# When a buffer of B and C counts as free in a fused attention and state-space kernel

## The chip, the cores and the metric

The kernel runs on one core of one Trainium2 chip. The metric is device time in microseconds of one execution, and the median of several runs is compared. Everything is float32.

## The reference, cut to what matters

The input is a batch of 4 images with 128 channels of 64 by 64 pixels. Layer 0 is attention with 4 heads of 32 channels over the 4096 pixels of an image, with residual and layer norm. Layer 1 adds a 3 by 3 convolution, a spectral mixing (an FFT, a 1 by 1 convolution, the inverse FFT) and a Mamba block. The Mamba block is where the change sits:

```python
x_dbl = einsum('blr of xs and x_proj_w')
dt = softplus(x_dbl[..., :8] @ dt_proj_w + dt_proj_b)
Bm, Cm = x_dbl[..., 8:24], x_dbl[..., 24:]
# for every pixel t in order, 256 channels d, 16 states n
dA = exp(dt[..., None] * A)
h = dA * h + dt[..., None] * Bt[:, None, :] * xt[..., None]
y = einsum('bdn,bn->bd', h, Ct)
```

B and C are one number for each pixel and state, shared by all channels. The kernel holds channels on the partitions, so each row of B and C has to be copied to all 128 partitions.

## The kernel before

**Tiling.** The pixels are cut into 32 chunks of 512 (L), 8 for each image. Attention runs in 64 halves (HALVES): a chunk of queries and a pair of heads, against 32 tiles of 128 keys (NT). The state space is scanned chunk by chunk, in 32 scans for each chunk: 16 states n times 2 halves of the 256 channels.

**One loop orders everything.** The program is written out by a loop over a step t. Step t of a half makes the scores for one tile of keys, takes their exponentials and multiplies the previous ones with the values; it also makes the scores whose maxima the next half needs (`scores_for_max`, reduced by VectorE on L473). Jobs such as projections, the convolution, normalising and stores are generators that a small planner (`Plan.step`) advances by one piece in a step. The main loop passes t = 2048 when attention ends; the steps after that have only scans and jobs, and this text calls them the tail. All queues run in the order of this text. SP issues nearly all DMAs, one queue for all of them.

**The scan.** A state takes four steps. For scan v of a chunk (v = 2n for the first half of the channels, 2n + 1 for the second) and a step counted from the chunk's start:
- at odd steps, two scans ahead, `scan_input_term` (L845) multiplies B into the input: db. GpSimd does it, VectorE in the tail.
- at even steps, `scan_state` runs the recurrence on VectorE (L857), copies the last column as the carried state (L866, GpSimd), multiplies the result by C (L867, GpSimd) and adds it up (L886 on GpSimd; in the tail TensorE adds through a product with the identity, L893).
- at odd steps, after the input term, the loop may issue one `scan_load`: the rows of B and C of one state, copied to all partitions, 512 KB in one DMA (L823).

The first use of a load is db of the first half (L845), its last use is the product of the second half on L867, "the last product". Load n is first used 3 steps before its first scan, and its last product stands at local step 4n + 2.

**Buffers.** Three buffers named bc go round in turn; `ring[0]` counts the free ones. From step 2017 on, tiles of K and V that attention no longer needs are handed over as well (`spare`), each taking two DMAs (L829); they come back six steps after their last product. `scan_load` takes a ring buffer first. The wait itself is not in this code: the framework makes the DMA wait on SP until the last reader of the buffer, the product on L867, has ended.

**Who stands behind a load on SP.** Every half sends its row maxima through memory: `maxima` stores them (L485) and reads them back one step later as 16 small DMAs (L492, tile MX). `normalise` sends sums of exponentials the same way (L554 and L556, then L559 reading tile zc, VectorE's reciprocal on L562, L564, L567). `flips` loads a partial output into the single buffer ob (L1057) and the mirrored term wr (L994), adds them on GpSimd (L1003, L1004) and stores (L1064). In the text these stand between loads of B and C, as the steps fall.

Of the kernel before, what the change touches and what calls it, by code (L numbers as in the profile page):

```python
# [161 lines left out]
def attention_then_conv_mamba(  # L162
# [21 lines left out]
    NT = N // P  # L184
# [154 lines left out]
    plan = Plan(2, {"x": 2, "f": 1})  # L339
# [114 lines left out]
    def scores_for_max(H, s):  # L454

        k = H % PAIRS
        m, t = divmod(s, TPC)
        assert have["K", k, m] == H // PAIRS // NCH
        if s == 0:
            part[H] = att.tile([P, 2, TPC, NCH], F32, tag="part", name=f"part_{H}")  # L460

        tag = "s2" if H == 0 and s % 2 else "s1"
        sc = psum.tile([P, 2, L], F32, tag=tag, name=f"s1_{H}_{s}")
        for n in range(2):
            for j in range(2):
                nc.tensor.matmul(  # L466
                    sc[:, j, :],
                    QT[H][rows[j], n, t * P : (t + 1) * P],
                    KK[k][m][rows[j], :],
                    start=n == 0,  # L470
                    stop=n == 1,
                )
        nc.vector.tensor_reduce(part[H][:, :, t, m], sc, AX.X, ALU.max)  # L473
# [25 lines left out]
    def scores_for_exp(H, m):  # L499

        k = H % PAIRS
        i, t = divmod(m, TPC)
        assert have["K", k, i] == H // PAIRS // NCH
        s = psum.tile([P, 2, L], F32, tag="s2", name=f"s2_{H}_{m}")
        for n, mov in enumerate((QT[H][:, 0, :], QT[H][:, 1, :], MX[H])):
            for j in range(2):
                nc.tensor.matmul(  # L507
                    s[:, j, :],
                    sel[rows[j], :] if n == 2 else KK[k][i][rows[j], t * P : (t + 1) * P],
                    mov[rows[j], :],  # L510
                    start=n == 0,
                    stop=n == 2,
                )
        e = att.tile([P, 2, L], F32, tag="e", name=f"e_{H}_{m}", bufs=3)
        nc.scalar.activation(e, s, AF.Exp)  # L515
        es[H, m] = e

    def times_values(H, m):

        k = H % PAIRS  # L520
        i, t = divmod(m, TPC)
        assert have["V", i] == H // PAIRS // NCH
        if m == 0:
            po[H] = psum.tile([P, L], F32, tag="o", name=f"po_{H}")
        e = es.pop((H, m))
        for j in range(2):
            nc.tensor.matmul(  # L527
                po[H][used[j], :],
                VA[i][:, t, 2 * k + j, :],
                e[:, j, :],  # L530
                start=m == 0,
                stop=m == NT - 1,
            )
        if m == NT - 1:
            p = po.pop(H)
            oz[H] = att.tile([P, L], F32, tag="oz", name=f"oz_{H}", bufs=1)
            nc.scalar.activation(oz[H][used[0], :], p[used[0], :], AF.Identity)
            nc.vector.tensor_copy(oz[H][used[1], :], p[used[1], :])  # L538
# [271 lines left out]
    spare = [((HALVES - 1) * NT + 1, KK[0][i : i + 2]) for i in range(0, NCH, 2)]  # L810
    spare += [(HALVES * NT + 12, KK[1][i : i + 2]) for i in range(0, NCH, 2)]
    spare += [(HALVES * NT + 20, VA[i : i + 2]) for i in range(4, NCH, 2)]
    taken, ring = {}, [3]

    def flat(t):
        return t.bitcast(F32) if len(t.shape) == 2 else t.rearrange("p t h d -> p (t h d)")[:, :L]

    def scan_load(c, n):

        if ring[0]:  # L820
            ring[0] -= 1
            bc = loc.tile([P, 2, L], F32, tag="bc", name=f"bc_{c}_{n}", bufs=3)
            nc.sync.dma_start(bc, bcds[c][n::NS, :].partition_broadcast(P))  # L823
            bcs[c, n] = [bc[:, k, :] for k in range(2)]
        else:
            taken[c, n] = spare.pop(0)[1]
            bcs[c, n] = [flat(t) for t in taken[c, n]]
            for k in range(2):
                nc.sync.dma_start(  # L829
                    bcs[c, n][k].unsqueeze(1),  # L830
                    bcds[c][k * NS + n : k * NS + n + 1, :].partition_broadcast(P),
                )

    def scan_decay(c, v):
        n, hf = divmod(v, NH)
        k = hf * NS + n

        tag = "o" if plan.t >= HALVES * NT + 2 and v % 2 else "dA"
        dA[c, v] = psum.tile([P, L], F32, tag=tag, name=f"dA_{c}_{k}")
        nc.scalar.activation(dA[c, v], dts[c][hf], AF.Exp, scale=negA[:, k : k + 1])  # L840

    def scan_input_term(c, v, engine):
        n, hf = divmod(v, NH)
        db[c, v] = loc.tile([P, L], F32, tag="db", name=f"db_{c}_{hf * NS + n}")
        engine.tensor_tensor(db[c, v], us[c][hf], bcs[c, n][0], ALU.mult)  # L845

    def scan_state(c, v):

        n, hf = divmod(v, NH)
        k = hf * NS + n  # L850
        assert (c, hf) in scaled
        late = plan.t > HALVES * NT + 1
        if late:
            hs = flat(VA[v % 4])
        else:
            hs = loc.tile([P, L], F32, tag="hs", name=f"hs_{c}_{k}")
        nc.vector.tensor_tensor_scan(  # L857
            hs,
            dA.pop((c, v)),
            db.pop((c, v)),  # L860
            state[:, k : k + 1] if c % NCH else zero,
            ALU.mult,
            ALU.add,
        )
        if c % NCH < NCH - 1:
            nc.gpsimd.tensor_copy(state[:, k : k + 1], hs[:, L - 1 :])  # L866
        nc.gpsimd.tensor_tensor(hs, hs, bcs[c, n][1], ALU.mult)  # L867
        if hf == NH - 1 and (c, n) in taken:
            spare.append((plan.t + 6, taken.pop((c, n))))
        elif hf == NH - 1:  # L870
            ring[0] += 1
        if late:

            if c not in sums_late:
                sums_late[c] = psum.tile(
                    [P, NH, L], F32, tag=f"s{1 + c % 2}", name=f"acc_{c}"
                )
            terms = [hs] if n else [xss[c][hf], hs]
            for x in terms:
                waiting.append((plan.t + 4, c, hf, x, n == NS - 1 and x is hs))  # L880
        elif n == 0:
            acc = loc.tile([P, L], F32, tag=f"acc{hf}", name=f"acc_{c}_{hf}")
            accs[c, hf] = acc
            nc.gpsimd.tensor_tensor(acc, xss[c][hf], hs, ALU.add)
        else:
            nc.gpsimd.tensor_tensor(accs[c, hf], accs[c, hf], hs, ALU.add)  # L886
# [217 lines left out]
    t = 6 - SLOT  # L1104
    loaded = 0
    end = (CHUNKS + 3) * SLOT
    while t < end or not plan.idle():
        H, m = divmod(t, NT)
        if 0 <= H < HALVES:
            scores_for_exp(H, m)  # L1110
        h1, s1 = divmod(t + LEAD, NT)
        if 0 <= h1 + 1 < HALVES:
            scores_for_max(h1 + 1, s1)
        H, m = divmod(t - 1, NT)
        last = m == NT - 1
        if last and 0 <= H < HALVES:
            times_values(H, m)
        c, s = divmod(t - LAG, SLOT)
        odd = s % 2 == 1
        if -1 <= c < CHUNKS:  # L1120
            v = c * STATES + s // 2
            if not odd:
                if v >= 0:
                    scan_state(*divmod(v, STATES))
            else:
                if 0 <= v + 1 < CHUNKS * STATES:
                    scan_decay(*divmod(v + 1, STATES))
                if 0 <= v + 2 < CHUNKS * STATES:
                    late = t > HALVES * NT
                    scan_input_term(  # L1130
                        *divmod(v + 2, STATES), nc.vector if late else nc.gpsimd
                    )

                if loaded < CHUNKS * NS and loaded // NS in bcds:
                    if ring[0] or spare and spare[0][0] <= t:
                        scan_load(*divmod(loaded, NS))
                        loaded += 1
        plan.late = t > HALVES * NT
        if plan.late:
            add_states()  # L1140
            if odd:
                plan.step(t, {"D": 4, "P": 4, "A": 6})
            plan.t = t
        elif t < -LEAD:
            plan.step(t, {"D": 4, "P": 4, "A": 4})
        elif odd:
            plan.step(t, {"D": 2, "P": 2, "A": 2})
        else:
            plan.step(t, {"D": 0, "P": 0, "A": 1})
        if not last and 0 <= H < HALVES:  # L1150
            times_values(H, m)
        t += 1
# [76 lines left out]
```

## Time and profile before

| what | value |
|---|---|
| median of 3 runs | 5970.94 us (5969.76 to 5976.89) |
| the profiled execution's own time | 5976.93 us |
| its span, first to last instruction | 5975.1 us |
| TensorE busy | 5766.0 us, 96% of the span |
| GpSimd busy | 4575.5 us, 77% |
| VectorE busy | 4343.8 us, 73% |
| ScalarE busy | 3535.4 us, 59% |
| loads of B and C into bc | 487, 512 KB each |
| DMAs through K and V tiles (L829) | 50, 256 KB each |
| granted TensorE clock | 0.985 over the span |

The span has a start of some 160 us, attention to about 5745 us, and the tail. A table of busy time by stretches gives TensorE 990.40 us of 1000 between 1000 and 2000 us, and 9.94 of 20 between 5760 and 5780 us. So the same wait has a different worth in the two stretches. In the table of waits the idle time of an engine stands before the instruction that ended it, with the instruction or the DMA that released it. SP's own waits are listed apart: standing there costs time only if something behind in its queue is missed by an engine.

### The profile page before, as it was taken

The page shows a single profiled execution, that of the slowest core. Times are in us where ns is not written, and L with a number is a line of the kernel's source. Part 1 is how long each engine was busy: PE and PEld are TensorE (multiplying, and loading weights), DVE is VectorE, ACT ScalarE, POOL GpSimd, SP SyncE. Part 2 cuts the span into 40 slices and gives each one's busy share as a digit, 9 for nine tenths or more (in the row PEclk, how much of TensorE's full clock was granted, in tenths as well). Part 3 has the DMA queues.
Part 4 walks back from the last instruction along what each step waited for, and adds up shares of the span by engine and source line. Part 5 has one row for each costly group of instructions (what it writes and reads, how often), then busy time and mean ns, then how long its engine had stood idle before and what let it go on. Part 6 is the DMA issues. An engine that isn't in the chain of part 4 may idle for free. (4 is left out here: it accounts for less than half of the span.)

```text
span 5975.1 us, 84571 instructions
## 1 busy us (share of the span) xinstructions
PE 5766.0 (96%) x31318; PEld 2461.1 (41%) x31318; DVE 4343.8 (73%) x4633; ACT 3535.4 (59%) x4762; POOL 4575.5 (77%) x4657
## 2 busy tenths in 40 slices
PE   5999999999999999999999999999999999999976
PEld 2444444444444444444444444444444444444422
DVE  4557777777777777777777777777777777777657
ACT  1455666665666665666666666666566666666653
POOL 0006888888888888888788888887888888888887
PEclk7999999999999999999999999999999999999988
DMA  4012232323332222323433333222433322222232
GB/s 126 25 34 59 68 73 74 74 71 110 82 93 75 74 71 72 77 68 83 109 86 79 78 70 71 78 72 68 110 76 94 70 66 66 66 72 66 68 93 88
DMA packets 423324, 456.50 MB, mean 76 GB/s; under 512 B 203360, under 2 KB 204928, under 8 KB 422912
## 3 DMA queue, kind: packets, MB, share of 16 engines
q1 hardware_dynamic: 418256, 449.23, 29.6%
q8 instruction: 247, 4.05, 0.3%
q10 hardware_dynamic: 4656, 1.87, 0.1%
q14 instruction: 165, 1.35, 0.1%
HBM read 376.21 MB, written 66.32 MB: 74 GB/s over the span
## 5 line engine op out<-in xcount | busy, mean ns | idle before, releaser
L473 DVE TENSOR_REDUCE part<-s 128x2 f32<-128x1024 f32 x2048 | 2498.1, 1221 | 1340.5 <-PE s L466 1340.3
L515 ACT ACTIVATE e<-s 128x1024 f32<-128x1024 f32 x2048 | 2095.6, 1023 | 2117.1 <-PE s L507 2114.8
L527 PE MATMUL po<-e,V 128*33 128x512 f32 x8192 | 2182.5, 605 | 4.0 <-DVE oz L538 0.3
L507 PE MATMUL s<-Q,K 64*128 64x512 f32 x8192 | 1502.4, 444 | 12.7 <-ACT e L515 5.7
L466 PE MATMUL s<-K,Q 64*128 64x512 f32 x8192 | 1327.9, 401 | 57.8 <-DVE part L473 46.0
L867 POOL TENSOR_TENSOR hs<-hs,bc 128x512 f32<-128x512 f32 x948 | 1212.6, 1279 | 155.4 <-DVE hs L857 87.1
L507 PEld LDWEIGHTS s<-Q,K 64*128 64x128 f32 x8192 | 610.4, 185 | 1737.9 <-ACT e L515 1290.3
L845 POOL TENSOR_TENSOR db<-u,bc 128x512 f32<-128x512 f32 x948 | 1216.8, 1284 | 0.0
L886 POOL TENSOR_TENSOR acc<-acc,hs 128x512 f32<-128x512 f32 x894 | 1146.7, 1283 | 70.1
L857 DVE TENSOR_TENSOR_SCAN hs<-dA,state,db 128x512 f32<-128x512 f32 x826 | 1052.8, 1275 | 70.3 <-ACT dA L840 39.9
L466 PEld LDWEIGHTS s<-K,Q 64*128 64x128 f32 x8192 | 751.8, 186 | 330.4 <-DVE part L473 165.4
L507 PE MATMUL s<-MX,sel 64*128 64x512 f32 x4096 | 815.4, 393 | 0.0
L840 ACT ACTIVATE dA<-dt,negA 128x512 f32<-128x512 f32 x1024 | 703.3, 687 | 152.7 <-DVE V L857 85.8
L866 POOL COPY state<-hs 128x1 f32<-128x1 f32 x858 | 160.5, 187 | 654.4 <-DVE hs L857 654.4
L527 PEld LDWEIGHTS po<-e,V 128*33 128x33 f32 x8192 | 305.5, 109 | 846.8 <-issue 807.7
L507 PEld LDWEIGHTS s<-MX,sel 64*128 64x128 f32 x4096 | 391.2, 184 | 93.9
L962 PE MATMUL pf<-d,cw 128*128 128x256 f32 x768 | 199.1, 396 | 7.3 <-POOL d L944 7.3
L571 POOL TENSOR_TENSOR op<-op,rz 128x512 f32<-128x512 f32 x32 | 41.5, 1298 | 177.2 <-DMA rz<-rd 177.2
L962 PEld LDWEIGHTS pf<-d,cw 128*128 128x128 f32 x768 | 141.1, 193 | 73.0 <-issue 47.4
L857 DVE TENSOR_TENSOR_SCAN hs<-dA,zero,db 128x512 f32<-128x512 f32 x128 | 163.1, 1275 | 2.9 <-POOL db L845 2.6
L893 PE MATMUL acc<-V,cst 128*128 128x512 f32 x140 | 96.3, 795 | 61.7 <-POOL V L867 61.3
L725 POOL TENSOR_TENSOR xs<-xs,sg_x 128x512 f32<-128x512 f32 x64 | 82.2, 1285 | 74.5 <-ACT sg_x L649 74.5
(156 smaller groups left out, 3541.8 us busy)
## 6 DMA issues: line engine op xcount, KB each, us to landing
bc<-bcd SPq DMA_DIRECT2D x487, 512.0 KB
Q<-qd SPq DMA_DIRECT2D x256, 128.0 KB
K<-kd SPq DMA_DIRECT2D x64, 256.0 KB
MX<-md SPq DMA_DIRECT2D x1024, 0.5 KB
K<-bcd SPq DMA_DIRECT2D x42, 256.0 KB
vd<-vst SPq DMA_DIRECT2D x32, 264.0 KB
V<-vd SPq DMA_DIRECT2D x32, 264.0 KB
xq<-in_x SPq DMA_DIRECT2D x32, 256.0 KB
```

The costliest lines, as they stand in the source:

```text
L466: nc.tensor.matmul(sc[:, j, :], QT[H][rows[j], n, t * P : (t + 1) * P], KK[k][m][rows[j], :], start=n == 0, stop=n == 1,)
L473: nc.vector.tensor_reduce(part[H][:, :, t, m], sc, AX.X, ALU.max)
L507: nc.tensor.matmul(s[:, j, :], sel[rows[j], :] if n == 2 else KK[k][i][rows[j], t * P : (t + 1) * P], mov[rows[j], :], start=n == 0, stop= ...
L515: nc.scalar.activation(e, s, AF.Exp)
L527: nc.tensor.matmul(po[H][used[j], :], VA[i][:, t, 2 * k + j, :], e[:, j, :], start=m == 0, stop=m == NT - 1,)
L840: nc.scalar.activation(dA[c, v], dts[c][hf], AF.Exp, scale=negA[:, k : k + 1])
L845: engine.tensor_tensor(db[c, v], us[c][hf], bcs[c, n][0], ALU.mult)
L857: nc.vector.tensor_tensor_scan(hs, dA.pop((c, v)), db.pop((c, v)), state[:, k : k + 1] if c % NCH else zero, ALU.mult, ALU.add,)
L866: nc.gpsimd.tensor_copy(state[:, k : k + 1], hs[:, L - 1 :])
L867: nc.gpsimd.tensor_tensor(hs, hs, bcs[c, n][1], ALU.mult)
L886: nc.gpsimd.tensor_tensor(accs[c, hf], accs[c, hf], hs, ALU.add)
L962: nc.tensor.matmul(pf[:, k], taps[k][:, dx, :], d[:, k, :, dx : dx + W], start=dx == 0 and not outer, stop=q == 5 or dx == 2 and not outer,)
```

## The change

A ring buffer used to count as free at the text of its last product. Now it carries a due time, four steps behind, and the loop takes it when that time is reached. `ring` becomes a list of due times, three of them long past at the start. Inside the scan part of step t, `plan.t` is still t - 1, on both sides of the comparison.

```diff
-    taken, ring = {}, [3]
+    taken, ring = {}, [-NT] * 3
...
     def scan_load(c, n):
 
-        if ring[0]:
-            ring[0] -= 1
+        if ring and ring[0] <= plan.t:
+            ring.pop(0)
             bc = loc.tile([P, 2, L], F32, tag="bc", name=f"bc_{c}_{n}", bufs=3)
...
         elif hf == NH - 1:
-            ring[0] += 1
+            ring.append(plan.t + 4)
...
                 if loaded < CHUNKS * NS and loaded // NS in bcds:
-                    if ring[0] or spare and spare[0][0] <= t:
+                    if ring and ring[0] <= plan.t or spare and spare[0][0] <= t:
                         scan_load(*divmod(loaded, NS))
                         loaded += 1
```

The number of buffers, the loads, the products and the spare tiles' own rule stay as they are.

## The prediction

> **What bounds the kernel now.** First the page: which engine is full. Then the table of waits, for PE and for SP's queue.
>
> ```profile
> PE 5766.0 (96%) x31318; PEld 2461.1 (41%) x31318; DVE 4343.8 (73%) x4633; ACT 3535.4 (59%) x4762; POOL 4575.5 (77%) x4657
> ```
>
> ```profile
> PE s L466 <- DVE part L473: 46.0, 88, 1.3
> ```
>
> ```profile
> SPq L823 <- POOL hs L867: 2795.0, 421, 29.5
> ```
>
> The last line is what the change aims at: SP stood 421 times, 6.6 us each, before a load whose buffer POOL was still reading. But until about 5745 us PE is 99% busy (990.40 of 1000 us between 1000 and 2000), and PE's stretches of idleness in attention come from DVE's maxima, not from a DMA. So I looked, after the first 480 us, for every idle stretch of a compute engine that a DMA ended. There are five: three for K tiles (L466 on L397, 6.8 us in sum), and two in the tail. The K loads stand behind the store L391, which waits for ACT, not for a B-and-C load; they stay.
>
> The first of the two, by the timelines of SP, DVE and POOL:
>
> ```profile
> 5749.24 1.15 SPq L556 DMA_DIRECT2D op<-oz  x2
> 5762.40 0.39 SPq L823 DMA_DIRECT2D bc<-bcd  x1
> 5762.89 0.41 SPq L559 DMA_DIRECT2D zc<-zd  x1
> ```
>
> ```profile
> 5757.85 0.71 DVE L845 TENSOR_TENSOR db<-u,bc 128x512 f32<-128x512 f32 x1
> 5767.20 0.20 DVE L562 RECIPROCAL zc<-zc 128x8 f32<-128x8 f32 x1 [8.64 <-DMA zc<-zd]
> ```
>
> ```profile
> 5765.39 1.26 POOL L867 TENSOR_TENSOR V<-V,K 128x512 f32<-128x512 f32 x1
> 5769.40 0.70 POOL L866 COPY state<-V 128x1 f32<-128x1 f32 x1 [2.74 <-DVE V L857]
> ```
>
> SP is done with L556 at 5750.39, stands 12 us at a load, and the 4 KB zc goes out at 5762.89. It is 4.31 us on its way, behind 512 KB. DVE idles 8.64 us; POOL has old work until 5766.65 and idles only 2.74. The second one:
>
> ```profile
> 5871.60 0.37 SPq L823 DMA_DIRECT2D bc<-bcd  x1
> 5872.02 0.46 SPq L1064 DMA_DIRECT2D out<-ob  x1
> 5877.48 0.32 SPq L1057 DMA_DIRECT2D ob<-ymd  x1
> 5877.85 0.43 SPq L994 DMA_DIRECT2D wr<-wd  x1
> ```
>
> ```profile
> 5880.84 1.25 POOL L1003 TENSOR_TENSOR ob<-ob,wr 128x504 f32<-128x504 f32 x1 [3.46 <-DMA wr<-wd]
> ```
>
> The store of ob was ready at 5868.17, when L1004 ended, and stood until 5872.02; the next ob can be loaded only when it has landed, and POOL pays 3.46 us.
>
> **The change part by part.**
>
> *Text order.* In the steady part the last product stands at step 4n + 2 and its successor's load at 4n + 3. The due time is (t - 1) + 4, compared with t - 1, at odd steps only: the load moves to 4n + 7. Its first use is at 4n + 9, so a lead of six steps becomes two. Throughput stays: one load in four steps. Counted through the loop, 468 of 512 loads move by 4 steps; at the hand-over to spare tiles some move by 2 or 8, the last 16 by 0 to 4, and ring loads go from 487 to 486. So SP issues as many DMAs as before, one more in two pieces: 0.4 us of SP's own, hidden in its idle time.
>
> *What it takes away.* A moved load finds its product done, so SP no longer stands 2795 us. In attention nothing missed the DMAs behind: worth 0.
>
> In the tail, before zc at step 2051 stands now the load of 2043. Its buffer's product is long done, so it issues behind L556 at about 5750.5, zc at 5750.9, landing (4.3 us again) at 5755.3. DVE needs it at 5758.56: the idle 8.64 goes. But POOL has work until 5766.65 and saves 2.74 us. Its later multiply L571 (op) releases the projection (PE, L586), for which DVE idled 3.29 us before L589 at 5779.15. That chain starts earlier by POOL's 2.74, not by 8.64. What is late next: the load of 2051, now at 2059. It waits for the product of step 2054 (POOL, 5766.65), lands at about 5771.7, and DVE, running ahead, stands some 3 us for it; L589 follows only at 5776.4, so this costs nothing. Value: -2.7; between 0 (if that load lands over 2 us later) and -8.6 (if POOL's queue gave way too).
>
> For the second, the ring has turned by one: the load at 2111 takes the buffer whose product stands at 2106 instead of 2110, so it issues at about 5866.8, the store at 5868.2, ob and wr some 4.5 us earlier than before. POOL's 3.46 goes. Value: -3.5, between 0 and -3.5. Behind it the tail is one chain of DVE and POOL in fixed order, so it passes on. Sum of the tail: -6.2.
>
> *What it moves.* Each ring load is now behind the DMAs of four more steps. Nearly all are harmless: the slack between landing and first use (median 12.5 us before) stays above 5 us in three of four. Once in each half it matters: the load that stood before md and MX now stands behind MX.
>
> ```profile
> 3091.51 0.37 SPq L823 DMA_DIRECT2D bc<-bcd  x1
> 3091.93 0.46 SPq L485 DMA_DIRECT2D md<-neg  x1
> 3096.46 10.37 SPq L492 DMA_DIRECT2D MX<-md  x16
> 3106.89 1.51 SPq L348 DMA_DIRECT2D xq<-in_x  x1
> 3108.51 0.36 SPq L1064 DMA_DIRECT2D out<-ob  x1
> 3108.97 8.70 SPq L823 DMA_DIRECT2D bc<-bcd  x2
> ```
>
> ```profile
> 3110.52 1.29 POOL L845 TENSOR_TENSOR db<-u,bc 128x512 f32<-128x512 f32 x1
> ```
>
> The first row's load is first used at 3110.52. It would now issue at 3108.97 instead of 3091.51, and with the landing of loads in the trace's semaphore updates (median 5.0 us, 4.4 to 6.6 for nine in ten; 5.2 for the one that issued at 3108.97) arrive at 3114.1, 3.6 us late. Done so for all 467 loads before step 2000, 51 are late, 155 us in sum. This bound lets MX stay where it was. But md no longer has a fresh 512 KB ahead of it. An early half, before any such load, shows what that is worth:
>
> ```profile
> 268.49 0.34 SPq L485 DMA_DIRECT2D md<-neg  x1
> 269.96 11.13 SPq L492 DMA_DIRECT2D MX<-md  x16
> ```
>
> 1.47 us from md to MX instead of 4.53: MX comes 3.1 us earlier, in every second half 2 us more, since SP also stood before md there. With MX earlier, the load arrives at about 3111.0, 0.5 us late. Over all loads, with 2.0 us for md, 6 are late by 2.5 us in sum, and some 40 have under 1.5 us to spare.
>
> What lateness costs: db stands three steps ahead of its scan, and in one half of two POOL has gaps that take it up. In the other it has none for some 40 instructions, the delay reaches DVE's scan, the maxima queued behind it, and PE's next scores. Carrying the bound's delays through those rows gives 43 us at DVE and 15 us at PE. Value taken: +1, the 2.5 us being mostly absorbed; between 0 and +43.
>
> *A rule that bears on it.* The trace's 5.0 us can be set against the Trainium skill, page DMA: Bandwidth & Descriptors, section on the anatomy of one DMA: a fixed 2.0 us and bytes over 436 GB/s (fitted on the GpSimd path, while these go through SP). For 524,288 bytes that is an estimate of 3.2 us. By the rule the loads behind MX would be in time and the +1 would be 0; by the trace they are on the edge. The trace is used.
>
> *Sum.* 5975.1 - 6.2 + 1 = 5969.9 span; with the 1.8 us around it 5971.7 in a profiled execution like this one. That one stood 6.0 us above the median shown, so the median would be 5965.7.
>
> **The rivals.**
>
> *A, the forecast*: small tail gain, attention untouched. 5966, on its own between 5959 and 5972.
>
> *B, the tail pays in full.* DVE's 8.64 and POOL's 3.46 are both on the end's path: -12.1, 5958.8, down to 5953 if the copies on L866, 0.65 us beside a busy DVE against 0.18 alone, shorten too. For it: PE is no bound there. Against it: POOL is busy without a gap until 5766.65.
>
> *C, slower: the load behind MX.* One mechanism, once a half: db waits on POOL for a load that issued after 16 small DMAs. If md lands no sooner, +15 - 6.2 = +9: 5980; if all the lateness at DVE reaches PE, +43 - 6.2 = +37: 6008. It decides beyond the 0.2% when the loads of the full halves are late by some 1.2 us each: about 29 such halves must cost PE 0.6 us each, after a slack of about 0.5. For it: the margin is under 1.5 us and two steps are all the lead left. Against it: 1.47 against 4.53 us.
>
> *D, it does nothing*: zc stays late through something else, the other wait too: 5971.
>
> **How the numbers follow.** A measurement of this kernel can tell about 0.2%, 12 us, from no change. A 0.54, D 0.05: within it, 0.59. B 0.23: faster. C 0.18: slower. The range reaches from 5954, in B, to 5983, the lower part of C; about a tenth is left out on the upper side and a little on the lower one.
>
> **What would show it.** SP's wait L823 on L867 falls from 2795 us to under a few hundred, and L492 on md from 246 to about 100-150 us. DVE's 8.64 before L562 and POOL's 3.46 before L1003 are gone; a wait of about 3 us of DVE or less for a bc load appears near 5768. POOL shows few waits of L845 for a bc load in attention, under 1 us each. If they are some 30 to 60 with 2 us or more, and PE's wait for L473 has grown well over 46 us, C is right. If the tail after 5745 us is 10 us shorter or more, B is.

## The result, and the profile after

The changed kernel takes 5961.6 us (median of 14 runs, 5958.31 to 5967.64) against 5973.35 us for the kernel before in the same comparison: a ratio of 0.9981 (95% interval 0.9973 to 0.9989), 11.7 us faster. The profiled execution has a span of 5956.5 us, 18.6 less than the one shown of before; 7 us of that difference are the scatter of single executions.

SP's own waits first, as the table of waits gives them for the changed kernel (waiting line and releaser, us in total, times, longest):

```profile
SPq L823 <- POOL hs L867: 997.3, 159, 29.5
SPq L485 <- DVE neg L482: 568.1, 64, 39.0
SPq L492 <- DMA md<-neg: 72.0, 64, 2.5
```

The last of these rows stood so before:

```profile
SPq L492 <- DMA md<-neg: 246.0, 64, 4.8
```

Standing at a load fell from 2795.0 to 997.3 us. SP now stands at the head of md's chain until VectorE has the maxima ready (L485), and it waits for md before MX 72.0 us instead of 246.0 over 64 halves: 1.1 us each instead of 3.8. Next, where the tail used to wait for zc: SP's timeline, then VectorE's.

```profile
5742.16 1.15 SPq L556 DMA_DIRECT2D op<-oz  x2
5743.40 0.53 SPq L823 DMA_DIRECT2D bc<-bcd  x1
5744.04 0.43 SPq L559 DMA_DIRECT2D zc<-zd  x1
...
5760.50 0.38 SPq L823 DMA_DIRECT2D bc<-bcd  x1
```

```profile
5751.37 0.19 DVE L562 RECIPROCAL zc<-zc 128x8 f32<-128x8 f32 x1
5753.78 0.88 DVE L977 SCALAR_TENSOR_TENSOR ym<-pf,vec,ym 128x256 f32<-128x256 f32 x2 [2.21 <-PE pf L962]
...
5760.78 1.28 DVE L857 TENSOR_TENSOR_SCAN V<-dA,state,db 128x512 f32<-128x512 f32 x1 [1.69 <-PE acc L893]
5765.44 1.21 DVE L845 TENSOR_TENSOR db<-u,bc 128x512 f32<-128x512 f32 x1 [3.38 <-DMA bc<-bcd]
```

zc goes out right behind L556, and the reciprocal has no wait. But most of the 8.64 us comes back as three other waits of VectorE: 2.21 us for the convolution, 1.69 for a scan buffer that TensorE has not added yet, and 3.38 for the load of 5760.50, which the change put behind zc. And the other place, SP and then GpSimd:

```profile
5852.22 0.37 SPq L823 DMA_DIRECT2D bc<-bcd  x1
5853.61 0.34 SPq L1064 DMA_DIRECT2D out<-ob  x1
5858.07 0.32 SPq L1057 DMA_DIRECT2D ob<-ymd  x1
5858.44 1.26 SPq L994 DMA_DIRECT2D wr<-wd  x1
```

```profile
5862.74 1.70 POOL L1003 TENSOR_TENSOR ob<-ob,wr 128x504 f32<-128x504 f32 x1
```

The store is no longer held up by a load, and L1003 starts as soon as GpSimd is free. The price that the prediction looked for is there as well. The page's row of POOL's input term, before and after, and one case of it with the SP rows that lead to it:

```profile
L845 POOL TENSOR_TENSOR db<-u,bc 128x512 f32<-128x512 f32 x948 | 1216.8, 1284 | 0.0
L845 POOL TENSOR_TENSOR db<-u,bc 128x512 f32<-128x512 f32 x946 | 1212.1, 1281 | 6.6 <-DMA bc<-bcd 5.8
```

```profile
1665.14 10.93 SPq L492 DMA_DIRECT2D MX<-md  x16
1676.12 0.59 SPq L348 DMA_DIRECT2D xq<-in_x  x1
1676.80 0.38 SPq L1064 DMA_DIRECT2D out<-ob  x1
1677.22 1.02 SPq L823 DMA_DIRECT2D bc<-bcd  x2
```

```profile
1683.44 1.27 POOL L845 TENSOR_TENSOR db<-u,bc 128x512 f32<-128x512 f32 x1 [1.30 <-DMA bc<-bcd]
```

That is 5.8 us of late loads in the whole of attention. When the instructions of both profiles are laid side by side, this one stands out: the changed kernel's lead shrinks by 1.3 us around 1683 us. The same comparison finds steps of 0.5, 4.0 and 2.2 us in its favour at the three places where one image's keys give way to the next one's, and 11.7 us in the tail (what of this is chance is told below).

Those three places are what the prediction set aside. TensorE waits there for a K tile. Here the middle one, before and after, with the timeline of TensorE, then the busy time by stretches (PEclk, third from the end, is the granted clock):

```profile
2897.60 0.74 PE L466 MATMUL s<-K,Q 64*128 64x512 f32 x4 [3.55 <-DMA K<-kd]
2898.27 2.59 PE L737 MATMUL pd<-xs,xpw 128*64 128x512 f32 x3
```

```profile
2897.60:2901.60 4.00, 4.00 (x11) 1.22 (x12) 1.82 (x2) 0.00 (x0) 1.18 (x1) 0.62 0.79 241
```

```profile
2894.30 0.73 PE L466 MATMUL s<-K,Q 64*128 64x512 f32 x4 [1.23 <-DMA K<-kd]
2894.96 1.50 PE L737 MATMUL pd<-xs,xpw 128*64 128x512 f32 x3
```

```profile
2894.00:2898.00 4.00, 3.70 (x14) 1.32 (x16) 1.82 (x2) 0.72 (x2) 3.73 (x3) 1.00 0.89 229
```

The wait is 2.3 us shorter, and there is a second price that no table of waits shows: behind the long one the granted clock is 0.62 for 4 us, and the same group of matmuls takes 2.59 instead of 1.50 us. Together the place is 4.0 us shorter.

SP's rows that lead to this tile, a load of B and C, the reads of Q and the K tile, before and then after:

```profile
2884.36 0.37 SPq L823 DMA_DIRECT2D bc<-bcd  x1
2884.78 3.03 SPq L446 DMA_DIRECT2D Q<-qd  x4
...
2892.60 0.32 SPq L397 DMA_DIRECT2D K<-kd  x1
```

```profile
2879.61 0.94 SPq L823 DMA_DIRECT2D bc<-bcd  x1
2880.61 2.39 SPq L446 DMA_DIRECT2D Q<-qd  x4
...
2890.94 0.44 SPq L397 DMA_DIRECT2D K<-kd  x1
```

Before, the reads of Q go out 7.8 us ahead of the tile, after it 10.3 us. The 3 us in front of the tile's issue show what the DMA engines still move then (the last number is GB/s):

```profile
2889.60:2892.60 3.00, 3.00 (x19) 1.15 (x18) 0.40 (x1) 1.54 (x3) 2.92 (x5) 1.00 0.91 226
```

```profile
2887.94:2890.94 3.00, 3.00 (x17) 1.08 (x15) 0.25 (x1) 1.52 (x4) 2.76 (x4) 1.00 0.30 97
```

### The profile page after: what moved, and what is told of

Same layout as the page of the kernel before. It is cut to its first block, busy times and chain, and to the rows that moved or that the text cites. A ratio compares the mean times of both kernels' runs of the same rounds, so it can differ in the third digit from the quotient of the medians.

```text
span 5956.5 us, 84545 instructions
## 1 busy us (share of the span) xinstructions
PE 5755.6 (97%) x31318; PEld 2455.5 (41%) x31318; DVE 4343.8 (73%) x4633; ACT 3533.2 (59%) x4762; POOL 4570.0 (77%) x4657
## 5 line engine op out<-in xcount | busy, mean ns | idle before, releaser
L515 ACT ACTIVATE e<-s 128x1024 f32<-128x1024 f32 x2048 | 2093.5, 1022 | 2110.7 <-PE s L507 2108.4
L466 PE MATMUL s<-K,Q 64*128 64x512 f32 x8192 | 1324.6, 400 | 57.6 <-DVE part L473 49.0
L867 POOL TENSOR_TENSOR hs<-hs,bc 128x512 f32<-128x512 f32 x946 | 1208.4, 1277 | 154.2 <-DVE hs L857 85.8
L845 POOL TENSOR_TENSOR db<-u,bc 128x512 f32<-128x512 f32 x946 | 1212.1, 1281 | 6.6 <-DMA bc<-bcd 5.8
L466 PEld LDWEIGHTS s<-K,Q 64*128 64x128 f32 x8192 | 749.6, 185 | 328.4 <-DVE part L473 165.7
```

The costliest lines, as they stand in the source:

```text
L466: nc.tensor.matmul(sc[:, j, :], QT[H][rows[j], n, t * P : (t + 1) * P], KK[k][m][rows[j], :], start=n == 0, stop=n == 1,)
```

## The experiments

Theory 1: the tail gives what its two waits gave, and the waits for K tiles with the clock behind them give the rest. Theory 2: the shifts in attention are chance. Rival C is the prediction's load behind MX.

**Half of the change each (e_att, e_tail).** Four steps for one side of step 1990, none for the other:

```diff
-            ring.append(plan.t + 4)
+            ring.append(plan.t + (4 if plan.t < 1990 else 0))   # e_att
+            ring.append(plan.t + (0 if plan.t < 1990 else 4))   # e_tail
```

> Four steps behind for the loads of attention alone (before step 1990), the old rule in the tail. Theory 1 (the tail brings what the tail showed, and three waits for K tiles at image boundaries bring the rest): 2 to 6 us faster than before, the two tail waits (8.64 us before L562, 3.46 us before L1003) are still there. Theory 2 (attention has no part, the boundary shifts are chance from run to run): within 2 us of before. Rival C (the load behind MX): slower by 1 us or more.

> The old rule up to step 1990, four steps behind from there. Theory 1: 6 to 9 us faster than before, both tail waits gone. Theory 2 (all of it in the tail): 11 to 12 us faster. Forecast of the prediction for the tail: 6.2 us. No wait of POOL L845 for a bc load in attention in any case.

Attention alone: 5967.83 us, ratio 0.9992 (0.9984 to 1.0000), 5.7 us faster by the medians and 4.8 by the ratio. The tail alone: 5966.23 us, 0.9989 (0.9982 to 0.9995), 7.3 and 6.6 us faster. Their sum, 13.0 or 11.4, is the whole change within the intervals. Attention has a part, with theory 1 and against theory 2; rival C's sign does not appear. The first interval only just reaches no change, so the profiles below have to carry it.

**Which loads in attention (e_k).** Four steps only for loads freed shortly before an image boundary:

```diff
+            ring.append(plan.t + (4 if plan.t < 1600 and 470 <= plan.t % 512 else 0))
```

> Four steps behind only for the loads freed within 42 steps ahead of the three image boundaries (some 30 of 512 loads), the old rule elsewhere. Theory 1 (K waits plus the TensorE clock that falls after them): first to last exponential 4 to 5 us shorter than before's 5610 us, K waits of L466 about 3.5 us in sum instead of 7, granted clock 1.00 in the 4 us behind each; 4 us faster by the median, and the tail as before (230 us). Theory 2 (the attention gain is spread over all loads): 0 to 1 us.

5967.37 us, ratio 0.9991 (0.9985 to 0.9998), 5.1 us faster: these few loads bring what all of attention brings. The expectation that its tail would be that of before was wrong (226.2 against 230.3 us, see below). The ten profiles without extra reads together: waits of L466 for K at the three boundaries, from the first exponential's start (L515) to the last one's, and from there to the end, in us:

| kernel | K waits | attention | tail |
|---|---|---|---|
| before | 1.38, 3.55, 1.85 | 5612.0 | 230.3 |
| e_zc | 1.37, 2.74, 2.96 | 5610.8 | 226.1 |
| e_wr | 1.62, 3.00, 1.90 | 5608.3 | 226.5 |
| e_tail | 1.00, 3.88, 3.45 | 5615.0 | 219.0 |
| changed | 0.89, 1.23, 1.27 | 5607.2 | 218.7 |
| changed again (e_after2) | 1.54, 2.72, 1.47 | 5609.7 | 222.2 |
| e_att | 0.93, 1.72, 1.06 | 5607.3 | 230.9 |
| e_k | 1.11, 1.01, 0.94 | 5605.4 | 226.2 |
| e_lag2 | 0.99, 0.97, 0.89 | 5604.8 | 223.7 |
| e_best | 0.96, 1.44, 1.41 | 5606.1 | 222.3 |

The first four have the old rule at the boundaries, with 7.2 us of K waits on average; the other six have 3.8. The sums do not overlap (6.5 to 8.3 against 2.9 to 5.7), but single waits do: the middle one of the changed kernel's repeat is 2.72 us, that of e_zc 2.74. Attention is 5611.5 us on average in the first and 5606.8 in the others: 4.8 us. Of that 3.4 are the waits.

The clock is the next term. Three exponentials around a K wait take 10.15 us plus the wait, to 0.02 us, in every case with the clock at 1.00 behind it. In the five cases where it fell they take 1.6 to 2.6 us more, all five with the old rule: 2.3 us for each of the four kernels on average. The late loads are the third. Take its K waits and its falls from each kernel's attention: seven kernels are left with 5601.8 to 5602.3 us, and the three that have four steps behind in all of attention with 5603.6 to 5604.0. So late loads cost these three about 1.7 us, and nothing else of size is left to explain.

The dearest, in e_tail, by stretches:

```profile
4321.60:4325.60 4.00, 3.95 (x10) 1.45 (x11) 1.82 (x2) 0.00 (x0) 1.33 (x2) 0.50 0.74 237
```

What decides on a fall can be read from the traces. The granted clock changes only on a grid of 3.41 us. Here are the stretches of that grid around the 1.85 us wait of before, and around a 3.00 us wait of e_wr, with TensorE's busy time in each; the third number from the end is the clock:

```profile
4318.49:4321.91 3.42, 1.57 (x12) 1.00 0.58 208
4321.91:4325.32 3.41, 3.41 (x8) 0.50 0.43 101
```

```profile
2889.91:2893.32 3.41, 1.81 (x10) 1.00 0.92 291
2893.32:2896.74 3.42, 2.02 (x9) 1.00 0.30 95
2896.74:2900.15 3.41, 3.41 (x20) 1.00 0.68 238
```

The shorter wait lies in one stretch and leaves it busy for 1.57 of 3.42 us; the next stretch has half the clock. The longer one is shared out over two stretches, each busy for more than half, and nothing falls. In attention of the ten profiles, from 200 us on, this holds without exception: half the clock followed each of the five stretches in which TensorE idled for 52% or more, and none of 8254 with 51% or less. (In the tail the border is less sharp, between 39 and 55%.) One stretch at half the clock is 1.7 us lost, which is the price of four of the five falls; the fall in e_tail by the 3.45 us wait lasted two.

**The two waits of the tail, each alone (e_zc, e_wr).** The kernel before with a single load held back by two steps:

```diff
-                if loaded < CHUNKS * NS and loaded // NS in bcds:
+                if loaded < CHUNKS * NS and loaded // NS in bcds and t != 2051:   # e_zc; 2111 in e_wr
```

> The kernel before, with the one load of step 2051 held back to step 2053, so that it stands behind zc on SP. The prediction's step (POOL's queue sets it): 2.7 us faster, POOL idle before L866 near 5769 gone. Rival B (DVE's wait pays in full): 8.6 us faster. Its attention is that of the kernel before, so its waits of L466 for K tiles at the three image boundaries tell whether 1.4, 3.6 and 1.9 us repeat (theory 1) or differ at random by 2 us (theory 2).

> The kernel before, with the one load of step 2111 held back to step 2113, so that the store of ob at 2111 is ahead of it on SP. The prediction's step: POOL's 3.46 us before L1003 gone and 3.5 us faster. If the tail behind it waits for something else: 0 to 1 us. Attention again as in the kernel before, for the K waits.

The medians, 5969.60 (ratio 0.9995, 0.9987 to 1.0003) and 5969.59 (0.9996, 0.9988 to 1.0004), do not tell 4 us from nothing; the profiles do. Counted from the last exponential's start, VectorE reaches the end of this place 2.8 us earlier in e_zc than before and 3.6 earlier in the changed kernel: the prediction's 2.7, not rival B's 8.6. (The K waits of e_zc repeat those of before at the first boundary only, so single K waits scatter by about 1 us.) In e_wr GpSimd's wait shrinks from 3.46 to 1.38 us, since its load at 2113 still stands before L1057, and VectorE gains 2.8 there; with four steps the wait is gone and the gain is 4.0.

```profile
5871.60 1.25 POOL L1003 TENSOR_TENSOR ob<-ob,wr 128x504 f32<-128x504 f32 x1 [1.38 <-DMA wr<-wd]
```

**The rest of the tail.** In the two profiles the tail differs by 11.7 us, and 3.6 and 4.0 leave about 4 of them. They sit at the last convolution. Its matmuls before, in e_k, whose tail is the same program, and in the repeat of the changed kernel:

```profile
5843.48 4.82 PE L962 MATMUL pf<-d,cw 128*128 128x256 f32 x12
```

```profile
5833.93 2.75 PE L962 MATMUL pf<-d,cw 128*128 128x256 f32 x12
```

```profile
5836.61 3.36 PE L962 MATMUL pf<-d,cw 128*128 128x256 f32 x12
```

The granted clock during these rows is 0.57, 1.00 and 0.82. Against before, VectorE gains 4 us at this place in the three profiles whose twelve matmuls take 2.75 us (changed, e_tail, e_k), and 1 us in the five where they take about 3.4. The same text runs at either speed from one execution to the next: e_k's tail is 226.2 us without any change in it, and the changed kernel's is 218.7 or 222.2. So by these runs this term is the clock's chance, and not the change's. Like compared with like, the tail falls from 226.2 (e_k) to 218.7 and 219.0 us at the fast speed, and from 230.9 (e_att) to 222.2 and 222.3 at 3.4 us: 7 to 9 us are the change's.

> The changed kernel once more, on the same chip as the mixed one: 11 to 12 us faster than before. K waits near 1 us each at full clock behind them, tail near 219 us; if the convolution's matmuls 93 us into the tail are slow here, the third term of the tail was chance.

The repeat is 5962.2 us, ratio 0.9982 (0.9975 to 0.9988), the first result again. Its K waits were not near 1 us each, as expected, but 1.54, 2.72 and 1.47.

**Lateness made large (e_mx2_after, e_mx2_before).** In both kernels 16 more reads of md behind MX, into memory that nothing reads:

```diff
+        aside = dram.tile([4 * TPC, P], F32, tag="aside", name=f"aside_{H}")
+        for j in range(2):
+            for r in range(2):
+                row = (2 * j + r) * TPC
+                for t in range(TPC):
+                    nc.sync.dma_start(aside[row + t : row + t + 1, :],
+                                      md[:, r, j, t : t + 1].rearrange("p o -> o p"))
```

> Four steps behind, with 16 more small reads of md behind the 16 of MX in each half (to memory, used by nothing): SP is busy 10 us longer there. Rival C's mechanism, doubled: the load behind MX is 9 to 10 us late in each of some 58 halves; POOL waits 500 us or more in sum, VectorE and TensorE inherit 4 to 8 us a half: 200 to 450 us slower than before. If lateness were absorbed by POOL's idle time, under 60 us slower.

> The kernel before with the same 16 more small reads in each half. The load ahead of md is not touched; the next one, 8.7 us to spare behind MX, is late by 1 to 2 us. Rival C's picture: 0 to 60 us slower than before, several times less than the kernel with four steps and the same reads. If the reads themselves cost something (queues, memory), both kernels slow down alike.

Both numbers were far off: 6912.15 us (ratio 1.1577, 1.1562 to 1.1593) and 6624.1 (1.1092, 1.1075 to 1.1109). The reads themselves are dearer than the 10 us of SP that I had counted; they also hold up the loads behind them and the queries' xq. What remains usable is POOL's waits, and with care the difference (changed kernel first; the input term is on L854 here):

```profile
POOL db L854 <- DMA bc<-bcd: 1095.2, 59, 22.5
DVE hs L866 <- POOL db L854: 894.8, 141, 17.7
PE pq L424 <- DMA xq<-in_x: 27.3, 3, 10.0
```

```profile
POOL db L854 <- DMA bc<-bcd: 589.7, 59, 14.6
DVE hs L866 <- POOL db L854: 208.3, 45, 12.9
PE pq L424 <- DMA xq<-in_x: 264.6, 31, 11.5
```

With the same reads the four steps make each of 59 loads 8.6 us later ((1095.2 - 589.7) / 59), near the expected 9 to 10, and the kernel 288 us slower, 4.9 us a half. So rival C's mechanism is real: VectorE's wait behind POOL grows from 208.3 to 894.8 us. What share of a large lateness reaches the end cannot be read off, because the kernel before pays 264.6 us for xq and the changed one only 27.3. In the changed kernel without the extra reads the lateness is 5.8 us in sum instead of 505.

**Other dues (e_lag2, e_best).** Two steps behind throughout, and two steps in attention with four in the tail:

```diff
+            ring.append(plan.t + 2)                                  # e_lag2
+            ring.append(plan.t + (2 if plan.t < 1990 else 4))        # e_best
```

> A due time two steps behind instead of four. The load that follows md in the text stays ahead of MX, so no POOL L845 waits for a bc load in attention (four steps: 5 waits of 0.4 to 1.7 us, of which one cost 1.3 us). K waits as with four steps. In the tail the load of 2051 goes to 2053, behind zc and on a buffer free earlier, so DVE's 3.4 us wait for it is gone too. Expected: 11 to 14 us faster than before, 0 to 2 us faster than four steps. If the lead of four steps were what matters on SP, 2 steps would bring half: 6 us.

> Two steps behind before step 1990, four from there. Attention as with two steps (first to last exponential near 5605 us), tail as with four (near 219 us). Theory (the terms are independent and add up): 13 to 18 us faster than before, 1 to 4 us faster than four steps throughout. If the tail's third term is the phase of the TensorE clock and no part of the change, the convolution's matmuls 93 to 99 us into the tail take 2.4 us or 3 to 4.5 us by chance, and the tail is 219 or 222 us.

e_lag2: 5960.38 us, ratio 0.9979 (0.9971 to 0.9987). No POOL L845 waits for a load, K waits are short, and DVE's 3.38 us in the tail is gone. e_best: 5960.52, ratio 0.9980 (0.9972 to 0.9988), 1.7 us under the changed kernel's repeat in the same comparison; the further 1 to 4 us expected are neither shown nor excluded. Its profile had a slow clock at the last convolution. None of the three is told from the others. Two steps have the same gain without late loads, so they are what I would keep; that they are faster is not shown.

## Why the prediction was right, and where it was not

The time lay in the range, and the sign was the forecast's. The size was not case A's: -5.2 was forecast, -11.7 measured, the size of rival B by another way. The range reached down to 5954 for rival B's sake, and B's mechanism did not happen, so that the measured time lay well inside it is in part luck. The sign set for B, a tail 10 us shorter or more, did appear in this pair of profiles (11.7), but about 4 us of it are the clock at the convolution. By the profiles the gain is 7 to 9 us in the tail and about 3.5 in attention: 2.9 of K waits and 2.3 of clock, less 1.7 for late loads (four steps in attention against the old rule, on average).

- *Text order, DMA count, ring by one turn*: as stated. POOL's wait before L1003 went.
- *The zc wait*: -2.7 forecast, -3.6 in the profile. POOL's queue did limit it, and the forecast new wait, "some 3 us", is the 3.38 us before L845 at 5765.44. Rival B's way, DVE's 8.64 in full, did not happen.
- *The wr wait*: -3.5 forecast, -4.0.
- *The load behind MX*: 6 late loads by 2.5 us in sum forecast; eight by 5.8 us in the changed kernel's profile, twelve by 7.7 in its repeat. "Under 1 us each" was too low (up to 1.68); the cost taken, +1, was about 1.7. The step that made the difference, md going to MX in 1.47 instead of 4.53 us, shows in L492's 72.0 us. The trace's landing of 5 us was the one to use, and not the 3.2 us estimated from the Trainium skill: by 3.2 us none of the eight would have been late, and seven of them took 4.9 to 6.2 us.
- *The step that failed*: "The K loads stand behind the store L391, which waits for ACT, not for a B-and-C load; they stay", worth 0. The order was right, the conclusion wrong. The tile at 2892.60 was 5.0 us on its way, behind four reads of Q that themselves stood behind a load; with Q gone earlier, the one at 2890.94 took 3.4. Over all boundaries the tile took 4.2 us on average with the old rule and 3.3 with the new, and in the 3 us before its issue the DMA engines moved 168 to 230 GB/s with the old rule and 64 to 142 with the new. SP's standing cost bandwidth at the wrong moment, not only order. That these loads are the cause is shown by e_k; that Q is what fills the engines is argued from the order, and the tile of the repeat that took 4.8 us at 84 GB/s is not explained. The term, put at 0, was -2.9 us of waits (the three kernels with four steps in attention against the four with the old rule, by the table), and the clock's -2.3 hangs on it.
- *The clock*: no step had it. The trace of before held a 3.55 us wait with a granted clock of 0.62 behind it, so the question could have been asked. The Trainium skill, page TensorE: Matmul & The Clock Gate, Part 1, says that TensorE's clock is halved after at least one idle window of about 3.4 us. It also says that the window runs freely, which agrees with the grid of 3.41 us here. By these words no fall was due, since TensorE was idle for 52 to 72% of the stretch ahead of each, and the clock's term would be 0; the traces show that half a stretch is enough, and they decide.
- *SP's wait on L867*, forecast under a few hundred us, is still 997.3: with nothing else in front, SP arrives early at the load. None of the engine waits shown above leads back to it; that it costs nothing is not tested.

## What to carry to other kernels

A wait on an in-order DMA queue costs what stands behind it, and also when the transfers behind it then move: for each wait that a large load postpones, look at how long the missed transfer was on its way, not only at when it was issued. Moving a prefetch later in the text frees the queue only as far as the lead lasts; find the longest burst that it is moved behind (here 16 small reads) and hold its landing against the first use. And where TensorE is full, ask of each of its waits whether it can cost clock as well: 1.85 us were enough here.

## What the runs showed of the hardware that was not expected

- TensorE's granted clock fell behind five of the nine K waits of 1.85 us or longer (behind all three of 3.45 us or more), and each fall cost 1.6 to 2.6 us on top of the wait. Not the length of the wait decided, but whether TensorE idled for more than half of one stretch of a 3.41 us grid: 1.85 us in one stretch were enough, 3.00 us over two were not.
- The last convolution's twelve matmuls took 2.75, 3.36 or 4.82 us for the same text, at a granted clock of 1.00, 0.82 and 0.57.
- A 256 KB tile of K took 3.0 to 5.6 us from issue to the end of TensorE's wait for it, on average 0.9 us longer where the DMA engines were busier in the 3 us ahead of it.
- 16 more reads of 4-byte elements (8 KB in all) into memory, once in each half, made the kernel before 652 us slower, about 10 us for each of the 64 halves.
